# Layer 0 window attention: softmax denominators out of the value products, inverted once a step and applied one step later

## The chip, the core and the metric

The kernel runs on one core of one Trainium2 chip. The metric is the device time of one execution in microseconds (us). TensorE, VectorE, ScalarE and GpSimd work in parallel beside SyncE, which issues DMA transfers; each engine works through its own list of instructions in order, and semaphores order the engines among each other. The profile calls them PE (and PEld for TensorE's weight loads), DVE, ACT, POOL and SP.

## What is computed

A chain of four layers on an image tensor of 4 x 16 x 512 x 512 float32 values. Layer 0 is a transformer block on windows of 8 x 8 pixels; layers 1 to 3 are 3x3 convolutions with batch normalisation, residuals and a small per-pixel network. The change lies wholly in layer 0:

```python
pos = conv3x3_depthwise(x); x = x + pos + pos_b
win = windows_of_8x8(affine(x))                 # 64 tokens, 16 channels
q, k, v = split(win @ qkv_w.T + qkv_b)          # 2 heads of 8
attn = softmax(q * 8**-0.5 @ k.T, axis=-1)
out = (attn @ v) @ proj_w.T + proj_b
x = x + out
x = x + gelu(affine(x) @ fc1_w.T + fc1_b) @ fc2_w.T + fc2_b
```

## The kernel before

**Tiling.** `window_attention` puts 8 strips of the image by 16 channels on the 128 partitions and walks over the image in `STEPS` = 64 steps. A step is 4 images (`u`) by 4 pairs of strips (`vv`) by 8 windows; two windows (the two strips of a pair) lie side by side on 128 token partitions. Within a step the attention runs over eight groups `k`, and the pieces of neighbouring groups are interleaved by hand. The order on PE, DVE, ACT and SP is the order in which the program writes the instructions (`manual_schedule`); only POOL is left to a scheduler.

**A group.** `scores(k)` multiplies keys and queries (L355) into four PSUM banks, 0 to 3, and two ACT instructions take the exponential of them into a tile `e` (L363). `values(k)` transposes the input on PE (L342) and DVE copies it to `yt` (L347). `attend(k-1)` makes 16 products of 128x32 tiles over 128 columns (L374: the weights are `yt`, whose half that belongs to the other window is zero) and then four of 128x32 tiles over 512 columns with a matrix of ones, `own` (L379). The latter are the softmax denominators, repeated over the 16 channels of each window. Even groups use banks 4 and 5, odd ones 6 and 7. `divide(k-1)` inverts the denominators on ACT as exp(-ln d) (L388, L389), and DVE multiplies products and inverses into `o` (L390).

**The rest of a step.** `turn_keys` copies keys of the next step from `y` to `y2` by DMA within SBUF, 8 transfers at every odd `k`, 32 a step, all on SP's queue (L314). `queries` prepares `g` for the next step (L324, L332, L334). `project` applies the output matrix and adds the residual (L398, L403). Then follows the hidden phase: 16 `hidden` blocks, products at L411 and a Gelu on ACT at L416, woven into the `depthwise` convolution (L291) of the step after next, whose result `position` writes to `y` (L302, L306). `output` multiplies by the second matrix (L422), DVE adds the residual into `xo` (L427). In every second step `store` writes `xo` to DRAM by 64 DMA transfers on SP's queue (L92). In the kernel before, all of `output` of a step is done early in the next step. The input tiles come by DMA as well (L190): 32 loads, one for two steps.

All DMA transfers use eight completion semaphores in turn, so that one is issued only after the transfer eight places ahead of it has landed.

Of the kernel before, what the change touches and what calls it, by code (L numbers as in the profile page):

```python
# [25 lines left out]
P = 128  # L26
# [122 lines left out]
def window_attention(ctx: ExitStack, tc, xw, x1, hots, m, v, peak):  # L149
# [33 lines left out]
    def quad(i):  # L183
        return slice(32 * i, 32 * i + 32)
# [1 line left out]
    xin = ctx.enter_context(tc.tile_pool(name="w0i", bufs=2))  # L186

    def load(k):
        t = xin.tile([P, V, WS + 2, XW + 2], F32, tag="x", name=f"x{k}")
        nc.sync.dma_start(t, xw[k])  # L190
        return t

    xts, ys = {0: load(0), 1: load(1)}, {}
    hot = wts.tile([P, 64], F32, name="hot")
    nc.sync.dma_start(hot, hots)
    small, own = hot[:, 0:32], hot[:, 32:64]

    def prod(lhsT, rhs, name, n=P):

# [73 lines left out]

    y2 = pa.tile([P, V, NJ, 2, T], F32, name="y2")
    nc.gpsimd.memset(y2, 0.0)
    g = pa.tile([P, V, NJ, NH, T], F32, name="g")
    o = pa.tile([P, V, NJ, NH, T], F32, name="o")
    most = pa.tile([P, STEPS], F32, name="most")

    def by_window(ap):  # L280
# [5 lines left out]
    def depthwise(n, tap, u):  # L286

        dy, dx = divmod(tap, 3)
        at = BW * (n % 2) + dx
        for vv in range(V):  # L290
            nc.tensor.matmul(  # L291
                bank(u)[quad(vv)], taps[quad(u), tap, :],
                xts[n // 2][quad(u), vv, dy : dy + WS, at : at + BW],
                start=tap == 0, stop=tap == 8,
            )

    def position(n):

        y = px.tile([P, U, N], F32, tag="y", name=f"y{n}", bufs=3)
# [37 lines left out]
    def values(k, n):  # L337

        vv, jl = k // 2, 4 * (k % 2)
        b = bank(4 + 2 * (k % 2))  # L340
        for jj in range(4):
            nc.tensor.transpose(  # L342
                b[:, P * jj : P * jj + P],
                y2[:, vv, jl + jj].rearrange("p w t -> p (w t)"), m("ident"),
            )
        t = px.tile([P, 4, P], F32, tag="yt", name=f"yt{n}_{k}", bufs=3)
        nc.vector.tensor_copy(t.rearrange("p j c -> p (j c)"), b)  # L347
        return t

    def scores(k, n):  # L350

        vv, jl = k // 2, 4 * (k % 2)
        for jj in range(4):
            for u in range(U):
                nc.tensor.matmul(  # L355
                    bank(u)[:, P * jj : P * jj + P],
                    y2[quad(u), vv, jl + jj].rearrange("p w t -> p (w t)"),
                    g[quad(u), vv, jl + jj].rearrange("p h t -> p (h t)"),
                    start=True, stop=True,
                )  # L360
        e = px.tile([P, U, 4, P], F32, tag="e", name=f"e{n}_{k}", bufs=3)
        for i in range(2):
            nc.scalar.activation(  # L363
                e[:, 2 * i : 2 * i + 2].rearrange("p u j t -> p u (j t)"),
                pairs[i], AF.Exp,
            )
        return e

    def attend(e, yt, k):

        b, d = bank(4 + 2 * (k % 2)), bank(5 + 2 * (k % 2))
        for jj in range(4):
            for u in range(U):
                nc.tensor.matmul(  # L374
                    b[quad(u), P * jj : P * jj + P], yt[:, jj, quad(u)], e[:, u, jj, :],
                    start=True, stop=True,
                )
        for u in range(U):
            nc.tensor.matmul(  # L379
                d[quad(u)], own, e[:, u].rearrange("p j t -> p (j t)"),  # L380
                start=True, stop=True,
            )

    def divide(k, n):
        vv, jl = k // 2, 4 * (k % 2)
        b, d = bank(4 + 2 * (k % 2)), bank(5 + 2 * (k % 2))
        r = px.tile([P, 512], F32, tag="r", name=f"r{n}_{k}")
        nc.scalar.activation(r, d, AF.Ln)  # L388
        nc.scalar.activation(r, r, AF.Exp, scale=-1.0)  # L389
        nc.vector.tensor_tensor(  # L390
            o[:, vv, jl : jl + 4].rearrange("p j h t -> p (j h t)"), b, r, ALU.mult
        )

    def project(y):
        for h in range(NH):
            for u in range(U):
                for vv in range(V):
                    nc.tensor.matmul(  # L398
                        bank(4 + u)[quad(vv)], wo[h][quad(u)], o[quad(u), vv, :, h, :],
                        start=h == 0, stop=h == 1,  # L400
                    )
        for u in range(U):
            nc.vector.scalar_tensor_tensor(  # L403
                y[:, u], bank(4 + u), pb, y[:, u], ALU.add, ALU.add
            )

    def hidden(y, q, vv, n):

        u, b = q // 4, bank(4 + q % 4)
        for k in range(4):  # L410
            nc.tensor.matmul(  # L411
                b[quad(k)], fc1[quad(vv), quad(k)], y[quad(vv), u, :],
                start=True, stop=True,
            )
        hd = px.tile([P, N], F32, tag="hid", name=f"hid{n}_{u}_{vv}", bufs=16)
        nc.scalar.activation(hd, b, AF.Gelu, bias=f1b)  # L416
        return vv, hd

# [61 lines left out]
    for n in range(2):  # L480
        for tap in range(9):
            for u in range(U):
                depthwise(n, tap, u)
        ys[n] = position(n)
    for vv in range(V):
        turn_keys(ys[0], vv)
    for h in range(NH):
        queries(ys[0], h)
    last, xo = None, None
    nc.scalar.preload_act_table_set("natural_log_exp_and_others")  # L490
    for n in range(STEPS):
        yts = {k: values(k, n) for k in range(2)}
        es = {0: scores(0, n)}
        if last:

            output(*last)
        for k in range(1, 8):
            es[k] = scores(k, n)
            attend(es[k - 1], yts[k - 1], k - 1)
            if k > 1:  # L500
                yts[k] = values(k, n)
            divide(k - 1, n)
            if k == 3:
                nc.vector.tensor_reduce(
                    most[:, n : n + 1], ys[n], AX.XY, ALU.max, apply_absolute_value=True
                )
            elif largest:
                largest.pop(0)()
            if k % 2 and n + 1 < STEPS:
                turn_keys(ys[n + 1], k // 2)  # L510
        if n + 1 < STEPS:
            queries(ys[n + 1], 0)
        attend(es[7], yts[7], 7)
        divide(7, n)
        if n + 1 < STEPS:
            queries(ys[n + 1], 1)
        y = ys.pop(n)
        project(y)

        ahead = n + 2 < STEPS  # L520
        if ahead and n % 2 == 0 and n // 2 + 2 < STEPS // 2:
            xts[n // 2 + 2] = load(n // 2 + 2)
        if n % 2 == 0:
            xo = px.tile([P, U, WS, XW], F32, tag="xo", name=f"xo{n}", bufs=1)
        if n + 1 == STEPS:
            flag = bounded()

# [3 lines left out]
        hids, taken = [], [0] * U  # L531
        for i in range(13 * 4):
            if i in at:
                q = len(hids)
                hids.append(hidden(y, q, i % 4, n))
                if n + 1 == STEPS and q in (5, 9, 13):
                    u = q // 4 - 1
                    output(y, xo, hids[q - 5 : q - 1], (u,), (u,), n)
            elif ahead:
                depthwise(n + 2, taken[i % 4], i % 4)  # L540
                taken[i % 4] += 1
        if n + 1 < STEPS:
# [3 lines left out]
        last = (y, xo, hids, range(U), (5, 7, 4, 6), n)  # L546
    output(y, xo, hids[12:], (3,), (3,), n)
    for f in largest:
        f()
    return nc.values_load(flag[0:1, 0:1], min_val=0, max_val=1)  # L550
# [676 lines left out]
def _pack(a):  # L1227
# [67 lines left out]
    own = np.zeros((2, 64, 2, C))  # L1295
    for w in range(2):
        own[w, :, w, :] = 1.0
    hots = np.concatenate(
        [np.tile(np.eye(32), (4, 1)), own.reshape(P, 32)], axis=1
    ).astype(np.float32)  # L1300


    padded = np.zeros((B, C, H + 2, W + 2), np.float32)
    padded[:, :, 1 : H + 1, 1 : W + 1] = a["x"]
    xw = np.zeros((WS, 4, B, 2, C, 4, WS + 2, P + 2), np.float32)
    for i in range(WS):
        for cb in range(4):
            for strip in range(8):
                vv, w = divmod(strip, 2)
                r = H // 8 * strip + WS * i  # L1310
                xw[i, cb, :, w, :, vv] = padded[
                    :, :, r : r + WS + 2, P * cb : P * cb + P + 2
                ]
    return {
        "x": a["x"].reshape(B * C, H, W),
        "xw": xw.reshape(4 * WS, P, 4, WS + 2, P + 2),
        "mats": mats,
        "vecs": vecs,
        "cqs": cws[:, 3].reshape(P, 6 * 32),
# [26 lines left out]
```

## Time and profile before

| | us |
|---|---|
| median of 3 runs | 6030.73 (6027.56 to 6033.05) |
| the profiled execution, its own time | 6030.1 |
| its span, first to last instruction | 6028.3 |
| PE busy | 5775.3 (96%) |
| ACT busy | 3837.6 (64%) |
| DVE busy | 3268.4 (54%) |
| POOL busy | 171.1 (3%) |
| granted TensorE clock, mean | 0.993 |

Layer 0 takes the first 3440 us or so of the span; the rest is layers 1 to 3. A row of the costliest groups reads: line, engine, operation, tile written <- tiles read, shapes, how many, busy us and mean ns of one, idle time of the engine before them and what ended it. SP's instructions are all issues and waits and do not count as busy: SP has no row in the first part of the page, and has to be read from the timeline and from the durations of its issues.

### The profile page before, as it was taken

The numbers are of one execution on the slowest core, as the hardware profiler recorded it, in microseconds if no ns is written. First come the engines' busy times: TensorE is split into PE (matmuls) and PEld (weight loads), VectorE is DVE, ScalarE is ACT, GpSimd is POOL, SyncE is SP. The second block draws the span as 40 slices with busy tenths as digits, with TensorE's granted clock in tenths as the row PEclk, the third lists the DMA queues.
The fourth block names the chain that finished last, engine by engine and source line by source line (L and its number), as shares of the span: only waits on it lengthen the run. The fifth ranks groups of instructions, "written<-read, shape, count | busy, mean of one in ns | idle before, by whom it ended". The sixth has DMA issues, their size and how long they took to land. (4 is left out here: it accounts for less than half of the span.)

```text
span 6028.3 us, 242228 instructions
## 1 busy us (share of the span) xinstructions
PE 5775.3 (96%) x108624; PEld 3084.9 (51%) x108624; DVE 3268.4 (54%) x4648; ACT 3837.6 (64%) x5257; POOL 171.1 (3%) x193
## 2 busy tenths in 40 slices
PE   8999999999999999999999866899999999999999
PEld 5666666666666666666666433333333333333333
DVE  3444444444444444444444455566666666666666
ACT  4777877877787777778777654344444444444444
POOL 0000000000000000000000154000000000000000
PEclk9999999999999999999999999999999999999999
DMA  3233333323333232333333398666676666666663
GB/s 84 58 71 66 64 77 62 78 59 71 67 64 77 61 79 59 71 66 65 77 61 61 58 243 216 163 171 168 167 173 165 168 172 166 168 171 168 167 170 104
DMA packets 638119, 674.57 MB, mean 112 GB/s; under 512 B 371728, under 2 KB 500880, under 8 KB 632976
## 3 DMA queue, kind: packets, MB, share of 16 engines
q1 hardware_dynamic: 635760, 657.53, 47.1%
q8 instruction: 857, 14.04, 1.0%
q0 software_dynamic: 1024, 1.05, 0.1%
q14 instruction: 190, 1.56, 0.1%
q10 hardware_dynamic: 288, 0.39, 0.0%
HBM read 221.15 MB, written 134.48 MB: 59 GB/s over the span
## 5 line engine op out<-in xcount | busy, mean ns | idle before, releaser
L363 ACT ACTIVATE e<-pair 128x1024 f32<-128x1024 f32 x1024 | 992.5, 1021 | 381.7 <-PE pair L355 381.7
L1175 ACT ACTIVATE hid<-tb,vec 128x512 f32<-128x512 f32 x1024 | 620.7, 688 | 517.5 <-PE tb L1167 517.4
L291 PE MATMUL pair<-x,taps 32*32 32x512 f32 x18432 | 927.4, 605 | 2.6 <-ACT y L302 1.2
L1177 DVE TENSOR_SCALAR hid<-tb,vec 128x512 f32<-128x512 f32 x1024 | 695.7, 742 | 2.7 <-PE tb L1167 2.6
L411 PE MATMUL bank<-y,fc_e 32*32 32x512 f32 x8192 | 680.1, 598 | 0.9 <-DVE y L403 0.9
L355 PE MATMUL pair<-g,y 32*128 32x128 f32 x16384 | 653.0, 285 | 26.9 <-ACT y L302 25.0
L355 PEld LDWEIGHTS pair<-g,y 32*128 32x128 f32 x16384 | 542.8, 186 | 215.9 <-issue 108.9
L416 ACT ACTIVATE hid<-bank,f1b 128x512 f32<-128x512 f32 x1024 | 644.5, 686 | 12.4 <-PE bank L411 4.8
L291 PEld LDWEIGHTS pair<-x,taps 32*32 32x32 f32 x18432 | 602.2, 103 | 98.2 <-issue 19.0
L347 DVE COPY yt<-bank 128x512 f32<-128x512 f32 x512 | 347.3, 688 | 540.2 <-PE bank L342 531.9
L1167 PE MATMUL tb<-ye,mat 32*128 32x512 f32 x4096 | 637.6, 624 | 0.3 <-DVE hid L1177 0.3
L374 PE MATMUL bank<-e,yt 128*32 128x128 f32 x16384 | 556.7, 276 | 3.4 <-issue 2.4
L390 DVE TENSOR_TENSOR o<-bank,r 128x512 f32<-128x512 f32 x512 | 354.2, 692 | 372.6 <-ACT r L389 356.3
L379 PE MATMUL bank<-e,hot 128*32 128x512 f32 x4096 | 535.6, 593 | 0.0
L1187 PE MATMUL tb<-hid,mat 128*32 128x512 f32 x4096 | 466.0, 595 | 41.6 <-DVE hid L1177 41.6
L374 PEld LDWEIGHTS bank<-e,yt 128*32 128x32 f32 x16384 | 418.0, 109 | 111.7 <-DVE yt L347 52.8
L306 DVE TENSOR_SCALAR y<-pair,vec 128x512 f32<-128x512 f32 x128 | 90.3, 746 | 706.5 <-PE pair L291 706.5
L1167 PEld LDWEIGHTS tb<-ye,mat 32*128 32x128 f32 x4096 | 267.0, 183 | 323.3 <-issue 219.9
L342 PEld LDWEIGHTS bank<-mat,y 128*128 128x128 f32 x2048 | 216.3, 141 | 376.1 <-issue 270.0
L1092 PE MATMUL tb<-zo,cw 64*32 64x512 f32 x3096 | 362.8, 594 | 14.9 <-issue 8.9
L1092 PE MATMUL tb<-xo,cw 64*32 64x512 f32 x3096 | 366.1, 600 | 10.1 <-issue 7.0
L1092 PE MATMUL tb<-xe,cw 64*32 64x512 f32 x3072 | 361.5, 600 | 0.0
(176 smaller groups left out, 7564.1 us busy)
## 6 DMA issues: line engine op xcount, KB each, us to landing
x<-in_xw_dram SPq DMA_DIRECT2D x32, 2600.0 KB, 10.9
zo<-ze SPq DMA_DIRECT2D x512, 128.5 KB, 2.4
ho<-he SPq DMA_DIRECT2D x512, 128.5 KB, 2.4
xo<-xe SPq DMA_DIRECT2D x512, 128.5 KB, 2.4
y<-y SPq DMA_DIRECT2D x2048, 32.0 KB, 2.2
tx<-x SPq DMA_DIRECT2D x256, 256.0 KB, 4.6
out_dram<-xe SPq DMA_DIRECT2D x128, 512.0 KB, 3.5
x<-xo SPq DMA_DIRECT2D x2016, 32.0 KB, 1.7
```

The costliest lines, as they stand in the source:

```text
L291: nc.tensor.matmul(bank(u)[quad(vv)], taps[quad(u), tap, :], xts[n // 2][quad(u), vv, dy : dy + WS, at : at + BW], start=tap == 0, stop=ta ...
L355: nc.tensor.matmul(bank(u)[:, P * jj : P * jj + P], y2[quad(u), vv, jl + jj].rearrange("p w t -> p (w t)"), g[quad(u), vv, jl + jj].rearra ...
L363: nc.scalar.activation(e[:, 2 * i : 2 * i + 2].rearrange("p u j t -> p u (j t)"), pairs[i], AF.Exp,)
L374: nc.tensor.matmul(b[quad(u), P * jj : P * jj + P], yt[:, jj, quad(u)], e[:, u, jj, :], start=True, stop=True,)
L379: nc.tensor.matmul(d[quad(u)], own, e[:, u].rearrange("p j t -> p (j t)"), start=True, stop=True,)
L411: nc.tensor.matmul(b[quad(k)], fc1[quad(vv), quad(k)], y[quad(vv), u, :], start=True, stop=True,)
L416: nc.scalar.activation(hd, b, AF.Gelu, bias=f1b)
L1092: nc.tensor.matmul(p[r][_quad(2 * f + w)], weights[_half(r), odd, dx, :], src[_half(r), f, dx : dx + W], start=dx == 0, stop=dx == 2,)
L1167: nc.tensor.matmul(p[q], w1[_quad(q), 1 - par, :], inner(src)[_quad(q), f, :], start=True, stop=True,)
L1175: nc.scalar.activation(hd, p[q], AF.Relu, bias=v("l3_b1"))
L1177: nc.vector.tensor_scalar(hd, p[q], v("l3_b1"), 0.0, ALU.add, ALU.max)
L1187: nc.tensor.matmul(p[r][_quad(c)], w2[:, par], hd, start=(r, c) not in seen, stop=(r, c) in seen,)
```

## The change

**Denominators.** The matrix of ones is no longer multiplied. Instead `values` adds a pattern `other` to the transposed block on DVE: ones in that half of the weights which was zero, the half of the other window's channels. `attend` makes 32 products of 64x32 tiles over 128 columns in place of 16 + 4 products: window 0 goes to the even bank of the pair, as 16 rows of values and 16 equal rows of sums; window 1 to the odd bank, as 16 rows of sums and 16 of values.

**Gathering.** For each group DVE copies both banks to SBUF (`o` and a new tile `t`, four buffers). Two DMA transfers take one row of sums for each image into a tile `sums` (4 x 2 KB each), and four transfers (`merge`, 16 x 2 KB each, one group later) carry window 1's values from `t` into `o`. All six are on SP's queue.

**Inversion.** ACT's logarithm and exponential work once a step on `sums`, at the start of the next step. There DVE spreads the inverse of each group over the partitions (`stream_shuffle` into `r`) and POOL multiplies it into `o`. So `project`, `hidden` and `output` of a step come one step later, and there is a 65th pass of the loop for the last.

**Buffers and order.** `o` has two buffers, `y` four in place of three, `e` two in place of three, `hid` eight in place of sixteen. Input tiles hold one step in place of two, so there are 64 loads of half the size. Half of `output` is done in the hidden phase, the other half early in the next step. The reductions for the largest values (`most`, `peak`) move from the groups to the time after `project`.

```diff
@@ values
-        nc.vector.tensor_copy(t.rearrange("p j c -> p (j c)"), b)
+        nc.vector.tensor_tensor(
+            t.rearrange("p j (u c) -> p (j u) c", u=U),
+            b.rearrange("p (a c) -> p a c", c=32),
+            other.unsqueeze(1).to_broadcast([P, 4 * U, 32]), ALU.add,
+        )
@@ attend
-        b, d = bank(4 + 2 * (k % 2)), bank(5 + 2 * (k % 2))
+        p = bank(4 + 2 * (k % 2)), bank(5 + 2 * (k % 2))
         for jj in range(4):
             for u in range(U):
-                nc.tensor.matmul(
-                    b[quad(u), P * jj : P * jj + P], yt[:, jj, quad(u)], e[:, u, jj, :],
-                    start=True, stop=True,
-                )
+                for w in range(2):
+                    half = slice(64 * w, 64 * w + 64)
+                    nc.tensor.matmul(
+                        p[w][quad(u), P * jj : P * jj + P],
+                        yt[half, jj, quad(u)], e[half, u, jj, :],
+                        start=True, stop=True,
+                    )
...
+    def gather(o, k, n):
+        b = part(o, k)
+        t = px.tile([P, 512], F32, tag="t", name=f"t{n}_{k}", bufs=4)
+        nc.vector.tensor_copy(b, bank(4 + 2 * (k % 2)))
+        nc.vector.tensor_copy(t, bank(5 + 2 * (k % 2)))
+        d = sums[n % 2]
+        nc.sync.dma_start(d[2 * k : P : 32], b[C:P:32])
+        nc.sync.dma_start(d[2 * k + 1 : P : 32], t[0:P:32])
+        merges.append((b, t))
+    def merge():
+        b, t = merges.pop(0)
         for u in range(U):
-            nc.tensor.matmul(
-                d[quad(u)], own, e[:, u].rearrange("p j t -> p (j t)"),
-                start=True, stop=True,
-            )
-    def divide(k, n):
-        vv, jl = k // 2, 4 * (k % 2)
-        b, d = bank(4 + 2 * (k % 2)), bank(5 + 2 * (k % 2))
+            at = slice(32 * u + C, 32 * u + 2 * C)
+            nc.sync.dma_start(b[at], t[at])
+    def invert(n):
+        d = sums[n % 2]
+        nc.scalar.activation(d, d, AF.Ln)
+        nc.scalar.activation(d, d, AF.Exp, scale=-1.0)
+    def divide(o, k, n):
         r = px.tile([P, 512], F32, tag="r", name=f"r{n}_{k}")
-        nc.scalar.activation(r, d, AF.Ln)
-        nc.scalar.activation(r, r, AF.Exp, scale=-1.0)
-        nc.vector.tensor_tensor(
-            o[:, vv, jl : jl + 4].rearrange("p j h t -> p (j h t)"), b, r, ALU.mult
-        )
+        nc.vector.stream_shuffle(r, sums[n % 2], [2 * k] * C + [2 * k + 1] * C)
+        b = part(o, k)
+        nc.gpsimd.tensor_tensor(b, b, r, ALU.mult)
@@ the loop over steps
+    for n in range(STEPS + 1):
+        old = os.get(n - 1)
...
         if last:
             output(*last)
+        if old is not None:
+            invert(n - 1)
+            divide(old, 0, n - 1)
         for k in range(1, 8):
+            if n < STEPS:
+                es[k] = scores(k, n)
+                attend(es[k - 1], yts[k - 1], k - 1)
+                if k > 1:
+                    yts[k] = values(k, n)
+                gather(o, k - 1, n)
+                if k > 1:
+                    merge()
+                if k % 2 and n + 1 < STEPS:
+                    turn_keys(ys[n + 1], k // 2)
+            if old is not None:
+                divide(old, k, n - 1)
         if n + 1 < STEPS:
             queries(ys[n + 1], 0)
-        attend(es[7], yts[7], 7)
-        divide(7, n)
+        if n < STEPS:
+            attend(es[7], yts[7], 7)
+            gather(o, 7, n)
+            for _ in range(2):
+                merge()
         if n + 1 < STEPS:
             queries(ys[n + 1], 1)
...
+                if q == 9:
+                    output(y, xo, hids[:8], (0, 1), (6, 7), done)
...
+        if loads:
+            xts[loads] = load(loads)
+        last = (y, xo, hids[8:], (2, 3), (5, 7), done) if old is not None else None
```

More of the change, by code (lines that the diff above doesn't have):

```diff
@@ L188, in load @@
     def load(k):
-        t = xin.tile([P, V, WS + 2, XW + 2], F32, tag="x", name=f"x{k}")
+        t = xin.tile([P, V, WS + 2, BW + 2], F32, tag="x", name=f"x{k}")
         nc.sync.dma_start(t, xw[k])
@@ L195, in window_attention @@
     nc.sync.dma_start(hot, hots)
-    small, own = hot[:, 0:32], hot[:, 32:64]
+    small, other = hot[:, 0:32], hot[:, 32:64]
     def prod(lhsT, rhs, name, n=P):
@@ L275, in window_attention @@
     nc.gpsimd.memset(y2, 0.0)
+    sums = [pa.tile([P, 512], F32, name=f"sums{i}") for i in range(2)]
+    for d in sums:
+        nc.gpsimd.memset(d, 1.0)
     g = pa.tile([P, V, NJ, NH, T], F32, name="g")
-    o = pa.tile([P, V, NJ, NH, T], F32, name="o")
     most = pa.tile([P, STEPS], F32, name="most")
@@ L288, in depthwise @@
         dy, dx = divmod(tap, 3)
-        at = BW * (n % 2) + dx
         for vv in range(V):
@@ L292, in depthwise @@
                 bank(u)[quad(vv)], taps[quad(u), tap, :],
-                xts[n // 2][quad(u), vv, dy : dy + WS, at : at + BW],
+                xts[n][quad(u), vv, dy : dy + WS, dx : dx + BW],
                 start=tap == 0, stop=tap == 8,
@@ L297, in position @@
     def position(n):
-        y = px.tile([P, U, N], F32, tag="y", name=f"y{n}", bufs=3)
+        y = px.tile([P, U, N], F32, tag="y", name=f"y{n}", bufs=4)
         for u in range(U):
@@ L360, in scores @@
                 )
-        e = px.tile([P, U, 4, P], F32, tag="e", name=f"e{n}_{k}", bufs=3)
+        e = px.tile([P, U, 4, P], F32, tag="e", name=f"e{n}_{k}", bufs=2)
         for i in range(2):
@@ new lines, in part @@
+    def part(o, k):
+        vv, jl = k // 2, 4 * (k % 2)
+        return o[:, vv, jl : jl + 4].rearrange("p j h t -> p (j h t)")
+    def gather(o, k, n):
[7 more added lines that the diff above has]
+        merges.append((b, t))
@@ L392, in divide, with highest, project @@
+    def highest(n):
+        nc.vector.tensor_reduce(
+            most[:, n : n + 1], ys[n], AX.XY, ALU.max, apply_absolute_value=True
         )
-    def project(y):
+    def project(y, o):
         for h in range(NH):
@@ L414, in hidden @@
             )
-        hd = px.tile([P, N], F32, tag="hid", name=f"hid{n}_{u}_{vv}", bufs=16)
+        hd = px.tile([P, N], F32, tag="hid", name=f"hid{n}_{u}_{vv}", bufs=8)
         nc.scalar.activation(hd, b, AF.Gelu, bias=f1b)
@@ L484, in window_attention @@
         ys[n] = position(n)
+        xts[n + 2] = load(n + 2)
     for vv in range(V):
@@ L488, in window_attention @@
         queries(ys[0], h)
-    last, xo = None, None
+    highest(0)
+    last, xo, os, merges = None, None, {}, []
     nc.scalar.preload_act_table_set("natural_log_exp_and_others")
-    for n in range(STEPS):
-        yts = {k: values(k, n) for k in range(2)}
-        es = {0: scores(0, n)}
+    for n in range(STEPS + 1):
+        old = os.get(n - 1)
+        if n < STEPS:
+            o = os[n] = pa.tile([P, V, NJ, NH, T], F32, tag="o", name=f"o{n}", bufs=2)
+            yts = {k: values(k, n) for k in range(2)}
+            es = {0: scores(0, n)}
@@ L494, in window_attention @@
         if last:
             output(*last)
+        if old is not None:
+            invert(n - 1)
+            divide(old, 0, n - 1)
         for k in range(1, 8):
[L498 to L505, printed above, removed]
-                )
-            elif largest:
-                largest.pop(0)()
@@ L509, in window_attention @@
-            if k % 2 and n + 1 < STEPS:
-                turn_keys(ys[n + 1], k // 2)
+            if n < STEPS:
[10 more added lines that the diff above has]
+                divide(old, k, n - 1)
@@ L511, in window_attention @@
         if n + 1 < STEPS:
             queries(ys[n + 1], 0)
-        attend(es[7], yts[7], 7)
-        divide(7, n)
+        if n < STEPS:
+            attend(es[7], yts[7], 7)
+            gather(o, 7, n)
+            for _ in range(2):
+                merge()
         if n + 1 < STEPS:
             queries(ys[n + 1], 1)
[L517 to L522, printed above, removed]
@@ L523, in window_attention @@
-        if n % 2 == 0:
-            xo = px.tile([P, U, WS, XW], F32, tag="xo", name=f"xo{n}", bufs=1)
         if n + 1 == STEPS:
             flag = bounded()
+        ahead = n + 2 < STEPS
+        if ahead and n + 4 < STEPS:
+            loads = n + 4
+        else:
+            loads = None
+        done = n - 1
+        if old is not None:
+            y = ys.pop(done)
+            project(y, os.pop(done))
+        if n + 1 < STEPS:
+            highest(n + 1)
+        if old is not None:
+            while largest:
+                largest.pop(0)()
+            if done % 2 == 0:
+                xo = px.tile([P, U, WS, XW], F32, tag="xo", name=f"xo{done}", bufs=1)
@@ L533, in window_attention @@
             if i in at:
+                if old is None:
+                    continue
                 q = len(hids)
[L535 to L538, printed above, removed]
+                hids.append(hidden(y, q, i % 4, done))
+                if q == 9:
+                    output(y, xo, hids[:8], (0, 1), (6, 7), done)
             elif ahead:
@@ L541, in window_attention @@
                 taken[i % 4] += 1
+            if i in (34, 44) and largest:
+                largest.pop(0)()
         if n + 1 < STEPS:
@@ L545, in window_attention @@
             ys[n + 2] = position(n + 2)
-        last = (y, xo, hids, range(U), (5, 7, 4, 6), n)
-    output(y, xo, hids[12:], (3,), (3,), n)
+        if loads:
+            xts[loads] = load(loads)
+        last = (y, xo, hids[8:], (2, 3), (5, 7), done) if old is not None else None
+    output(*last)
     for f in largest:
@@ L1293, in _pack @@
     cws = np.tile(np.concatenate([cws, cws[:, :, ::-1]]), (2, 1, 1, 1, 1))
-    own = np.zeros((2, 64, 2, C))
+    other = np.ones((2, 64, 2, C))
     for w in range(2):
-        own[w, :, w, :] = 1.0
+        other[w, :, w, :] = 0.0
     hots = np.concatenate(
-        [np.tile(np.eye(32), (4, 1)), own.reshape(P, 32)], axis=1
+        [np.tile(np.eye(32), (4, 1)), other.reshape(P, 32)], axis=1
     ).astype(np.float32)
@@ L1304, in _pack @@
     padded[:, :, 1 : H + 1, 1 : W + 1] = a["x"]
-    xw = np.zeros((WS, 4, B, 2, C, 4, WS + 2, P + 2), np.float32)
+    xw = np.zeros((WS, 8, B, 2, C, 4, WS + 2, P // 2 + 2), np.float32)
     for i in range(WS):
-        for cb in range(4):
+        for cb in range(8):
             for strip in range(8):
@@ L1311, in _pack @@
                 xw[i, cb, :, w, :, vv] = padded[
-                    :, :, r : r + WS + 2, P * cb : P * cb + P + 2
+                    :, :, r : r + WS + 2, P // 2 * cb : P // 2 * cb + P // 2 + 2
                 ]
@@ L1315, in _pack @@
         "x": a["x"].reshape(B * C, H, W),
-        "xw": xw.reshape(4 * WS, P, 4, WS + 2, P + 2),
+        "xw": xw.reshape(8 * WS, P, 4, WS + 2, P // 2 + 2),
         "mats": mats,
```

## The prediction

> **What bounds the kernel now.** I read the timeline of layer 0 first, because the change touches one group of a step and nothing after 3440 us. This is one group `k`:
>
> ```profile
> 1503.17 0.98 PEld L355 LDWEIGHTS pair<-g,y 32*128 32x128 f32 x32 [0.17 <-issue]
> ...
> 1504.27 1.08 PE L374 MATMUL bank<-e,yt 128*32 128x128 f32 x32
> 1504.38 1.94 ACT L363 ACTIVATE e<-pair 128x1024 f32<-128x1024 f32 x2 [0.40 <-PE pair L355]
> 1505.06 0.24 PEld L379 LDWEIGHTS bank<-e,hot 128*32 128x32 f32 x8
> ...
> 1506.14 0.42 PEld L342 LDWEIGHTS bank<-mat,y 128*128 128x128 f32 x4 [0.84 <-issue]
> ...
> 1506.28 0.60 ACT L388 ACTIVATE r<-bank 128x512 f32<-128x512 f32 x1
> 1506.73 0.98 PEld L355 LDWEIGHTS pair<-g,y 32*128 32x128 f32 x32 [0.17 <-issue]
> ```
>
> The group is 3.56 us from `scores` to `scores`, and PE goes from one product to the next: scores 1.10, values 0.79 (1504.27 to 1505.06), denominators 1.08 (to 1506.14), transposes 0.59. ACT idles 0.40 us in it, waiting for PE. So **PE is the bound of the groups**. The step's length comes from the instructions that read the projection, four a step:
>
> ```profile
> L403 DVE SCALAR_TENSOR_TENSOR y<-bank,pb,y x256: 739/743/752, 102.7 to 3426.4; 128x512 f32<-128x512 f32 x128
> ```
>
> From the first at 102.7 to the first of step 63 (3426.4 less 3 x 0.68) are 63 steps: **52.7 us a step**.
>
> Then I read SP, which has no busy row, because the change adds transfers. These are its issues, first in the lists by line (duration of one: least, median, most, in ns), then in the timeline of SP (start, length, how many):
>
> ```profile
> L314 SPq DMA_DIRECT2D y<-y x2048: 585/598/2127, 44.6 to 3401.1; - x187
> ```
> ```profile
> L92 SPq DMA_DIRECT2D x<-xo x2016: 302/424/2115, 175.7 to 3448.3; - x184
> ```
> ```profile
> L1037 SPq DMA_DIRECT2D zo<-ze x256: 507/590/1282, 3761.0 to 5938.7; - x128
> ```
> ```profile
> 1379.87 17.72 SPq L314 DMA_DIRECT2D y<-y  x24
> ...
> 1398.33 28.16 SPq L314 DMA_DIRECT2D y<-y  x32
> 1441.93 34.58 SPq L92 DMA_DIRECT2D x<-xo  x64
> ```
>
> An issue holds SP for 0.42 to 0.60 us, and some hold it over 2 us. With the gaps and the long ones, 24 `turn_keys` transfers took 17.72 us, 0.74 each; 64 stores took 34.58, and the next batch 36.12 (timeline at 1547): 0.55 each. Two steps hold 64 + 64 of them and one load at 0.6: 47.4 + 35.2 + 0.6 = **83.2 us of the 105.4 us of two steps**. SP is not a bound now, but it is 79% taken.
>
> [...] 0.60 us of issue against the 2.2 us that the page shows to landing, and issues follow one another while landings overlap. [...]
>
> **The change part by part.**
>
> *PE.* In L374 each column tile takes 8 of the 32 instructions in 0.79 us. The change has 64 instructions (every fp32 product is two) on eight tiles, again 8 on each: 0.79 us if eight run at once; 1.6 us if they only follow each other at L374's pace (0.79/32 each). The denominators' 1.08 us go. So PE's group falls from 3.56 to 2.5, at worst 3.3. I take 2.5.
>
> *ACT.* It loses L388 and L389, 8 x (0.596 + 0.630) = 9.8 us a step, and gains 1.2 once. But scores and exponential wait for each other: the banks 0 to 3 are single. At 1552.02 in the timeline `scores` of a group starts as the exponential before it ends, and the exponentials then stand 3.08 us apart (1550.28, 1553.36). So a group can't go below about 3.1 us, and PE's 1.08 is worth about 0.45 a group, 3 us over the seven of a step.
>
> *DVE.* Four instructions a group in place of two: the addition in `values` and two copies at 0.69 (L347's 688 ns, L390's 692), and the shuffle. [...]
>
> *POOL.* One product of two SBUF tiles a group. [...] The trace has only one-input work there (L980, 1024 columns in 1.12 us). It has a whole step of time; only above 6 us each would it matter.
>
> *SP.* Each group adds two transfers for `sums` and four for `merge`, 48 a step; loads double to one a step. No row shows 4 x 2 KB or 16 x 2 KB within SBUF. The nearest are layer 3's shifts within SBUF, 0.507 at least and 0.59 in the median. In the timeline at 5010 twelve of them start within 8.4 us, 0.70 each with waits; pairs without waits, 0.61 each. I take **0.66**, between these. The low end is a store's unstalled 0.47 (0.424 and the gap), say 0.5; the high end that of `turn_keys` at 0.74. Two steps then hold 47.4 + 35.2 + 1.2 + 96 x 0.66 = 63.4: **147.2 us of issues against 105.4 us that the steps last now.** That doesn't fit, so SP becomes the bound.
>
> *How it binds.* In SP's order a step is: two `sums` transfers, 8 `turn_keys`, then two and four, two and four and 8, and so on, 80 transfers, some 55 us, where the engines need 25 us for the groups. `t` has four buffers, so DVE's copy of group 6 waits for the merge of group 2, that of group 7 for the merge of group 3. Behind these copies stand, on DVE, the queries of the next step and the residual of `project`; PE waits for the banks, then ACT. After the merge of group 3 SP still has 38 transfers, 16 x 0.74 + 22 x 0.66 = 26.4, and a load. The engines take, from the copy of group 7 to the first `sums` transfer of the next step, what the trace shows from 1526.45 (end of L390) to about 1552.5: 26 us, plus the landing of 2.2. So in a step without stores SP rests 2 to 3 us; in a step with stores it never rests, as 32 of them are due in the hidden phase and 32 early in the next step, ahead of the first `sums` transfer. I add 3 us for this rest and 1.5 for waits behind the loads (1.3 MB; the 2.6 MB ones took 10.9 us to land): 151.7 us for two steps, **75.9 a step**.
>
> *Ends.* The 65th pass adds an inversion (1.2)[...] and about 4 of hidden work that no convolution covers: 15 us.
>
> *Sum.* 64 x (75.9 - 52.7) = 1485, and 15: 1500 over the profiled execution's 6030.1, that is **7530 us**. The median, 6030.73, is the same within 0.6.
>
> **The rivals.**
>
> *SP binds, at another price (part of the forecast).* At 0.5 us an issue: 47.4 + 35.2 + 1.2 + 48 + 3 = 134.8, 67.4 a step, 6985 us. At 0.74, with `turn_keys` at 0.78 and 6 us of rest: 50 + 35.2 + 1.2 + 71 + 7.5 = 164.9, 82.5 a step, 7950 us.[...]
>
> *Faster: SP keeps up.* Then the groups' 3 us a step are won: 6030 - 64 x 3 + 15 = 5850 us. For this the 96 transfers must fit into 2 x 49.7 - 83.8 = 15.6 us, 0.16 us each. The least issue of all rows is 0.302. I see nothing for it but that small transfers were never seen: 4%.
>
> *No gain, no loss.* 0.22 us an issue; no mechanism holds it there: 1%.
>
> *It doesn't do what it says.* If 64x32 products don't run eight at once, a group is 3.3 on PE instead of 3.1: under SP's bound this changes nothing, and without it it leaves about 6030 - 64 x 1.5 + 15 = 5950.
>
> *POOL or DVE binds.* Above 6 us for a POOL product the groups would take 8 x 6 and more. This would come on top only past SP's 75.9 a step, which needs 9 us each. I give it 2%, at 8000 and more.
>
> **How the numbers follow.** SP as the bound has 93%. Its own ends are 6985 and 7950; the likeliest value is 7530, and I give 7000 to 7900 for eight times in ten. A measurement of this kernel tells about 0.2%, 12 us, from no change. Faster 4%, same 1%, slower 95%.
>
> **What would show it.** Right: in the timeline SP's issues of layer 0 follow without a pause for most of a step; the new transfers' issue is 0.5 to 0.7; the first instruction of `project` comes every 76 us; PE's share in layer 0 falls to about 65%, and its long waits end on DVE's copy into `t` or on a DMA. The denominators' 1.08 us are gone, and PE's weights for 64x32 tiles take about 0.8 us a group. Wrong: issues at 0.3 or less, or a step below 60 us; a step of about 50 us means that SP kept up; long waits that end on POOL's product mean that POOL binds.

## The result, and the profile after

The changed kernel takes 7587.92 us in the median (7585.23 to 7591.73, four runs), the kernel before 6030.62 in the same comparison: a ratio of 1.2583, 95% interval 1.2561 to 1.2605. The profiled execution took 7591.7 us, its span is 7589.8, its mean granted clock 0.876 where it was 0.993.

The first two parts of the page after (busy time; then PE and the clock in 40 slices):

```profile
PE 5751.7 (76%) x120912; PEld 3145.4 (41%) x120912; DVE 3895.8 (51%) x6184; ACT 3315.0 (44%) x4363; POOL 822.0 (11%) x707
...
PE   7676676656675677656675676666899999999999
...
PEclk8888788878887888878887888779999999999999
```

Layer 0 fills the first 26 slices, and no engine reaches 80% in them. PE does about as many microseconds of work as before (5775.3) in a longer time. Something that has no busy row sets the end. The step, from the residual of `project` (least, median and most ns, first and last start):

```profile
L434 DVE SCALAR_TENSOR_TENSOR y<-bank,pb,y x256: 740/743/754, 170.1 to 4986.5; 128x512 f32<-128x512 f32 x128
```

(4986.5 - 3 x 0.68 - 170.1) / 63 = **76.4 us a step**. That is read as before. It is a mean of 63 unlike steps: in DVE's timeline they alternate, some 61 us without stores and some 94 with them, and the last one, in the 65th pass, which has no groups, took 35.7 (4948.83 to 4984.53). Without it the mean is 77.1. In the kernel before the steps take 52.7 to 54.3 us, and the last one 47.8. The timeline of SP, from one load to the load two steps later (start, length, how many):

```profile
1514.85 0.37 SPq L190 DMA_DIRECT2D x<-in_xw_dram  x1
1515.32 17.54 SPq L92 DMA_DIRECT2D x<-xo  x32
1532.96 0.56 SPq L398 DMA_DIRECT2D sums<-o  x1
1533.62 0.53 SPq L399 DMA_DIRECT2D sums<-t  x1
1534.26 5.39 SPq L315 DMA_DIRECT2D y<-y  x8
1539.74 0.57 SPq L398 DMA_DIRECT2D sums<-o  x1
1540.41 0.56 SPq L399 DMA_DIRECT2D sums<-t  x1
1541.07 2.48 SPq L406 DMA_DIRECT2D o<-t  x4
...
1581.62 5.55 SPq L406 DMA_DIRECT2D o<-t  x8
1587.27 0.53 SPq L190 DMA_DIRECT2D x<-in_xw_dram  x1
1590.42 0.55 SPq L398 DMA_DIRECT2D sums<-o  x1
...
1642.48 5.59 SPq L406 DMA_DIRECT2D o<-t  x8
1648.17 20.11 SPq L92 DMA_DIRECT2D x<-xo  x32
1668.38 0.37 SPq L190 DMA_DIRECT2D x<-in_xw_dram  x1
```

In these 153.5 us each transfer is issued at the end of the one before, mostly within 0.1 us. There is one rest of over half a microsecond, from 1587.80 to 1590.42, in the step that has no stores behind it. From 300 to 4800 us all gaps of over 0.3 us sum to 170 us, some 4% of the time, and waits for the landing of earlier transfers are among them. (In the kernel before, of 3207 issues from 300 to 3300 us none ends before the transfer eight places ahead of it has landed, and 26 before the one seven places ahead has.) So it is the issues themselves that fill the time: SP is the bound. The durations of its issues, by line:

```profile
L398 SPq DMA_DIRECT2D sums<-o x512: 503/563/637, 78.6 to 4950.0; - x171
```
```profile
L406 SPq DMA_DIRECT2D o<-t x2048: 527/587/1887, 87.2 to 4955.7; - x187
```

How the engines feel it is in the list of waits (us in total, times, longest us; 100 to 4990 us):

```profile
POOL o L418 <- DVE r L416: 3115.8, 371, 37.9
ACT g L333 <- DVE g L335: 1841.7, 126, 46.5
DVE t L396 <- DMA o<-t: 1560.0, 203, 36.0
PEld bank L381 <- DVE yt L348: 1041.9, 65, 35.0
```

The root is the third line: DVE's copy into `t` waits for a merge, 1560 us in 203 stops. Behind it on DVE stand `queries` (ACT's wait) and the addition into `yt` (PE's wait). The first line, the largest, is the idle time of an engine that is 11% busy and costs nothing.

Between the stops the groups run as follows. One group, in PE's weights:

```profile
1603.97 1.25 PEld L360 LDWEIGHTS pair<-g,y 32*128 32x128 f32 x32 [0.17 <-issue]
1605.34 0.91 PEld L381 LDWEIGHTS bank<-e,yt 64*32 64x32 f32 x64
1606.45 0.42 PEld L343 LDWEIGHTS bank<-mat,y 128*128 128x128 f32 x4 [0.20 <-issue]
1607.04 1.26 PEld L360 LDWEIGHTS pair<-g,y 32*128 32x128 f32 x32 [0.17 <-issue]
```

The denominators are gone and the group is 3.07 us long (1603.97 to 1607.04), against 3.56. The 64 products of 64x32 tiles take 1.11 us to the next transposes; in 0.20 of it no weights are loaded.

### The profile page after: what moved, and what is told of

Read it like the earlier page. It is cut to its first block, busy times and chain, and to the rows that moved or that the text cites. A ratio compares the mean times of both kernels' runs of the same rounds, so it can differ in the third digit from the quotient of the medians.

```text
span 7589.8 us, 274615 instructions
## 1 busy us (share of the span) xinstructions
PE 5751.7 (76%) x120912; PEld 3145.4 (41%) x120912; DVE 3895.8 (51%) x6184; ACT 3315.0 (44%) x4363; POOL 822.0 (11%) x707
## 5 line engine op out<-in xcount | busy, mean ns | idle before, releaser
L381 PE MATMUL bank<-e,yt 64*32 64x128 f32 x32768 | 641.1, 286 | 1039.1 <-DVE yt L348 1009.8
L396 DVE COPY t<-bank 128x512 f32<-128x512 f32 x512 | 351.1, 686 | 1572.1 <-DMA o<-t 1567.7
L418 POOL TENSOR_TENSOR o<-o,r 128x512 f32<-128x512 f32 x512 | 650.2, 1271 | 4298.1 <-DVE r L416 3115.8
L333 ACT ACTIVATE g<-pair,gb 128x512 f32<-128x512 f32 x256 | 172.4, 688 | 1847.8 <-DVE g L335 1847.8
L381 PEld LDWEIGHTS bank<-e,yt 64*32 64x32 f32 x32768 | 488.9, 110 | 1175.9 <-DVE yt L348 1046.9
L360 PE MATMUL pair<-g,y 32*128 32x128 f32 x16384 | 777.9, 290 | 50.5 <-ACT e L368 23.9
L360 PEld LDWEIGHTS pair<-g,y 32*128 32x128 f32 x16384 | 647.0, 188 | 222.2 <-ACT e L368 111.6
L325 PE MATMUL pair<-y,wg 32*32 32x512 f32 x4096 | 275.2, 915 | 514.9 <-ACT g L333 513.4
L348 DVE TENSOR_TENSOR yt<-bank,hot 128x512 f32<-128x512 f32 x512 | 346.6, 687 | 300.3 <-PE bank L343 298.1
L416 DVE STREAM_SHUFFLE r<-sums 128x512 f32<-128x512 f32 x512 | 375.0, 733 | 0.6
```

The lines of the kernel that those rows point to most:

```text
L360: nc.tensor.matmul(bank(u)[:, P * jj : P * jj + P], y2[quad(u), vv, jl + jj].rearrange("p w t -> p (w t)"), g[quad(u), vv, jl + jj].rearra ...
L381: nc.tensor.matmul(p[w][quad(u), P * jj : P * jj + P], yt[half, jj, quad(u)], e[half, u, jj, :], start=True, stop=True,)
L418: nc.gpsimd.tensor_tensor(b, b, r, ALU.mult)
```

## The experiments

In each kernel a step is the mean of 63 from the residual of `project`, as above; with the step of delay the last of them is a short one everywhere (35 to 37 us). The kernel before was run beside all of them (6024 to 6027 us in the median). A figure without a ratio is a single execution.

### The issues alone, without the change

The kernel before gets 48 transfers a step on SP, of the same shapes and in the same places, into a tile that nobody reads. `e` has two buffers in place of three, for room. 

```diff
+        nc.sync.dma_start(spare[2 * k : P : 32], src[C:P:32])
+        nc.sync.dma_start(spare[2 * k + 1 : P : 32], src[0:P:32])
...
+        for u in range(U):
+            at = slice(32 * u + C, 32 * u + 2 * C)
+            nc.sync.dma_start(spare2[at, k % 2], src[at])
```

> The kernel before, with 48 transfers a step of the same two sizes within SBUF added on SP's queue at the same places (two of 4 x 2 KB and four of 16 x 2 KB a group) into a spare tile that nobody reads; e has two buffers in place of three to make room. Theory A: SP's issues alone make 74.4 us a step and some rest: 6030 + 64 x 23 = 7500 us, 7350 to 7650. Theory B: nobody waits for these transfers, so only turn_keys come a little later: 6030 to 6150 us.

Measured: 7453.21 us, a step of 75.1. The change costs 1557 us, and the issues alone cost 1427, with four buffers of `t`, the inversion, POOL's products and the 64x32 products all absent. The wait is another one here (200 to 4800 us):

```profile
PE bank L344 <- DMA spare<-o: 486.0, 26, 20.1
```

L344 is the transposes of `values`, which read what `turn_keys` brought. In the timeline PE stops before them for 17 us, until 1600.46, and the eight `turn_keys` transfers that they need are issued from 1593.24 to 1598.64; the list puts the wait down to a spare transfer that was issued beside them. So nobody waits for `t` here, and the step is nearly the same: SP's queue sets it by whatever is waited for in the queue.

A smaller dose tells whether the cost is proportional or begins at a threshold: only the two transfers for `sums` a group, 16 a step.

```diff
-        for u in range(U):
-            at = slice(32 * u + C, 32 * u + 2 * C)
-            nc.sync.dma_start(spare2[at, k % 2], src[at])
```

> The kernel before with 16 transfers a step of 4 x 2 KB added on SP's queue, read by nobody (e with two buffers, as in e4). Theory A: 42 + 16 x 0.66 = 52.6 us a step on SP just reach the 52.7 us of the engines; with a rest 53.5 to 55.5 a step: 6080 to 6210 us. If each added issue cost its share of e4's loss whatever the room on SP (1427 us for 48): 6030 + 476 = 6500 us.

Measured: 6168.03 us, ratio 1.0248 (1.0221 to 1.0274), a step of 54.8. A third of the transfers costs a tenth of the loss. With 83.2 + 32 x 0.66 = 104.3 us of issues in two steps SP stands just at the 105.4 of the kernel before, so the cost begins at a threshold. In DVE's timeline the steps without stores still take 52.7 us, and only those with stores are longer (53.0 to 61.6). That also shows that the two buffers of `e` cost nothing in this kernel as long as SP keeps up.

### The change without its transfers

All 48 transfers a step are left out. So `sums` keeps ones and window 1's values are left out of the result. The work of PE, ACT, DVE and POOL is that of the change.

```diff
-        nc.sync.dma_start(d[2 * k : P : 32], b[C:P:32])
-        nc.sync.dma_start(d[2 * k + 1 : P : 32], t[0:P:32])
...
-            nc.sync.dma_start(b[at], t[at])
```

> The changed kernel without its 48 new transfers a step: left out are the gathering of the sums (sums stay ones, so nothing is divided) and window 1's values in o. All else of the change stays, on the same engines: 64x32 products, copies, inversion, shuffles, products on POOL, the step of delay. Theory A (only the issues made it slow): SP has its 42 us of before, and the engines set the step. From e7, where a step without a transfer in the way lasted 53.2 us, I expect 52 to 54 us a step: 6000 to 6150 us, within 2% of the kernel before. Theory B (the longer chain of inverting, shuffling and multiplying, or the products themselves): it stays above 6300 us.

Measured: 6058.43 us, ratio 1.0056 (1.004 to 1.0073), a step of 52.8. From the other side again: the transfers carry all of the loss but some 35 us (6058.43 less the 6023.76 beside it). But the 3 us a step that the groups should give don't appear either. The wait list of this kernel (200 to 3300 us), and of the kernel before, for the products of `attend`:

```profile
PE bank L381 <- issue: 59.0, 46, 3.3
```
```profile
PE bank L374 <- issue: 2.4, 4, 1.2
```

PE stops inside a burst of 64 products though the list shows nothing that it waits for. The timeline of one such stop, PE's weights:

```profile
1502.47 0.79 PEld L381 LDWEIGHTS bank<-e,yt 64*32 64x32 f32 x50
1506.12 0.22 PEld L381 LDWEIGHTS bank<-e,yt 64*32 64x32 f32 x14 [2.86 <-issue]
1506.72 0.71 PEld L343 LDWEIGHTS bank<-mat,y 128*128 128x128 f32 x4 [0.39 <-issue]
```

This stop costs more than its length: the granted clock is 1.00 from 1499.3 to 1502.5 and 0.57 from 1506 to 1510, and the weights of four transposes (L343) take 0.71 us in place of 0.42.

The DMA view of 1498 to 1508 has in it the input load of 1320 KB, which keeps the DMA engines over 90% busy for most of 1501.5 to 1505, and two packets of the queue that the page calls "instruction". This queue (q8) is read as the one that brings PE's instructions: it has 953 packets in this run and 857 in the kernel before, one for 254 instructions of PE and PEld in both. From 200 to 3300 us PE's weights stop 42 times for over 1 us with the reason "issue", and each stop ends 1.2 to 1.8 us after the end of a packet of this queue; a time chosen at random would lie so in 12 of 100 cases. So these stops are read as PE waiting for its instructions.

To see whether the load is what stops PE, the same kernel was run without input loads except the first two: the input of 62 steps is left out as well.

```diff
-            xts[loads] = load(loads)
+            xts[loads] = xts[loads - 2]
```

> As e11 (no new transfers), and without the loads of the input tiles but the first two: the convolutions of all later steps read these two again (left out: the input of 62 steps). In e11 PE stops in the middle of a group for 0.8 to 3.2 us in most steps and goes on at 'issue', while the DMA engines are busy with the 1.3 MB load of a step; steps without such a stop last 50.5 us, the mean 53.15. Theory C (the load in flight delays what PE needs to go on, its own instructions, fetched by DMA): the stops vanish, 50.5 to 51.5 us a step: 5890 to 5960 us, below the kernel before. If the stops come from the 64x32 products themselves: 6040 to 6080, as e11.

Measured: 5928.08 us, ratio 0.9831 (0.9816 to 0.9846), a step of 50.6. Its wait list, the same line:

```profile
PE bank L381 <- issue: 2.6, 6, 0.8
```

No stop of over 1 us is left. At the three lines of the groups (L381, L360, L343) PE's stops with the reason "issue" sum to 3.2 us, where the kernel with loads has 96.6. The time is 130 us less; the slower products behind each stop fit the rest, which was not taken apart.

The load alone is not enough. In the kernel before one of 2600 KB is in flight in the group that the prediction shows (the window, then PE, PEld, DVE, ACT and POOL busy, clock, DMA share, GB/s):

```profile
1503.17:1506.73 3.56, 3.56 (x77) 2.43 (x77) 1.38 (x2) 3.13 (x5) 0.00 (x0) 1.00 0.98 333
```

PE doesn't stop there. It has 152 instructions, weights and products, in the 3.56 us of that group; the changed one has 200 in 3.07. That PE uses its instructions up faster than they come in beside a load fits both; the time from the request of a packet to its landing was not seen. The kernel before was not run without its loads; PE is 99% busy in its layer 0 (3122.5 of 3150 us), so it has little to win there.

### More buffers for t

```diff
-        t = px.tile([P, 512], F32, tag="t", name=f"t{n}_{k}", bufs=4)
+        t = px.tile([P, 512], F32, tag="t", name=f"t{n}_{k}", bufs=6)
```

> The changed kernel with six buffers of t in place of four. Theory A (SP's issue time sets the step): the copies into t wait later, but SP has the same 149 us of issues in two steps; only the rest of 3 us in every second step can shrink: 7490 to 7600 us. Theory B' (the four buffers throttle the groups, and SP merely follows): two more groups run ahead, and 10 us or more a step are won: below 7000 us.

Measured: 7538.2 us, ratio 1.2506 (1.2482 to 1.2529), a step of 75.9. So the copies' wait for `t`, though it is the root in the wait list, is only where SP's delay comes in. Two more buffers take away part of SP's rest, 50 us: its gaps of over 0.3 us fall from 3.8 to 2.7% of the time (300 to 4700 us here). The rate of issue stays.

### Sharing the issues with POOL

Three kernels move part of SP's list to POOL's queue. The stores:

```diff
-                    slice(XW * cb, XW * cb + XW), queues if k == STEPS // 2 - 1 else None,
+                    slice(XW * cb, XW * cb + XW),
+                    queues if k == STEPS // 2 - 1 else itertools.repeat(nc.gpsimd),
```

> The changed kernel with the stores of xo (64 in two steps) issued from POOL's queue in place of SP's. Theory A (SP's issue time sets the step): SP keeps 112 issues less 32 a step: two steps hold 64 x 0.74 + 96 x 0.67 + 1.2 = 113 us of issues, 56.6 a step, with a rest of some 3 us a step before the first sums transfer 59.5 us a step; time about 7588 - 64 x (76.4 - 59.5) = 6510 us, 6400 to 6650. Theory B (the new waits set it: sums must land, be inverted, shuffled and multiplied before project[...]; SP's own load only goes along): nothing of that chain changes, 7400 to 7600 us.

Measured: 7000.32 us, a step of 67.0; 490 us more than expected. The timeline of POOL shows why:

```profile
1599.96 15.12 POOL L92 DMA_DIRECT2D x<-xo  x30 [15.83 <-DVE xo L458]
1616.36 0.51 POOL L92 DMA_DIRECT2D x<-xo  x1 [1.28 <-DMA x<-xo]
1617.56 16.60 POOL L92 DMA_DIRECT2D x<-xo  x33 [0.69 <-DMA x<-xo]
1634.18 3.72 POOL L418 TENSOR_TENSOR o<-o,r 128x512 f32<-128x512 f32 x3
```

POOL first waits for `xo`, then issues 64 stores until 1634.16, and only then come products. DVE's shuffle needs a buffer of `r` back from a product, so it waits too (475.9 us in 27 stops from 300 to 4000 us, up to 20.2). One queue was relieved and another, with work that is waited for, got a block of 34 us.

The merges, and then all 48 transfers, on POOL:

```diff
-            nc.sync.dma_start(b[at], t[at])
+            nc.gpsimd.dma_start(b[at], t[at])
```

> The changed kernel with the 32 merge transfers a step on POOL's queue. Theory A: SP has 32 x 0.74 + 32 x 0.55 + 16 x 0.66 + 0.6 = 52.5 us a step, with a rest 54 to 56; 7588 - 64 x 21.4 = 6220 us, 6100 to 6350. Theory B: the wait of DVE's copy into t for the merge stays, now for a transfer from POOL, 7400 us or more. If a POOL issue takes over 1 us, POOL has 32 + 10 us a step, still no bound.

Measured: 6746.69 us, a step of 63.2; over 500 us more than expected. POOL's merges can't run ahead of SP (300 to 4000 us):

```profile
POOL o L406 <- DMA sums<-o: 805.1, 166, 15.3
```

A merge overwrites rows of `o` behind the transfer that reads a row of sums from it, and that one still stands in SP's list behind the stores. In DVE's timeline the steps alternate, some 53 us without stores and 74 with them.

```diff
-        nc.sync.dma_start(d[2 * k : P : 32], b[C:P:32])
-        nc.sync.dma_start(d[2 * k + 1 : P : 32], t[0:P:32])
+        nc.gpsimd.dma_start(d[2 * k : P : 32], b[C:P:32])
+        nc.gpsimd.dma_start(d[2 * k + 1 : P : 32], t[0:P:32])
...
-            nc.sync.dma_start(b[at], t[at])
+            nc.gpsimd.dma_start(b[at], t[at])
```

> The changed kernel with all 48 new transfers a step on POOL's queue. Theory A: SP is back at 42 us a step, and the engines set the step: 50 to 51 us, so 7588 - 64 x 26 = 5925 us, 5850 to 6030, a little below the kernel before; POOL has 48 x 0.52 + 8 x 1.27 = 35 us a step. If an issue on POOL takes 1 us, POOL is the bound at 58 us a step: 6400 us. Theory B: 7400 us or more.

Measured: 6724.03 us, ratio 1.1147 (1.1128 to 1.1166), a step of 63.0. In SP's timeline there is now a rest of 6.5 us ahead of a load (1560.96 to 1567.44), 5.6 behind it and 21 after the next `turn_keys`, so SP no longer binds. POOL's timeline in the groups:

```profile
1528.04 2.01 POOL L406 DMA_DIRECT2D o<-t  x4 [0.91 <-DMA sums<-o]
1530.04 0.57 POOL L398 DMA_DIRECT2D sums<-o  x1
1530.61 0.57 POOL L399 DMA_DIRECT2D sums<-t  x1
1531.21 1.28 POOL L418 TENSOR_TENSOR o<-o,r 128x512 f32<-128x512 f32 x1
1533.37 2.01 POOL L406 DMA_DIRECT2D o<-t  x4 [0.88 <-DMA sums<-o]
```

A transfer holds POOL for 0.49 to 0.58 us in the median (merges, `sums`), much as it holds SP. A group is 2.01 + 2 x 0.57 + 1.28 = 4.4 us of POOL, and 5.3 with the waits for earlier transfers to land (0.91), against 3.1 on the other engines. POOL also releases `project`, in the wait list of this kernel (200 to 4000 us):

```profile
PEld bank L429 <- POOL o L418: 306.8, 60, 8.9
```

5.1 us in each step. So this is the prediction's sign of a bound by POOL, brought about by issues and not by the products, which kept their 1.28. That would be half of the 10.2 us by which the step exceeds that without transfers; the other half was not taken apart.

### Fewer, wider transfers

If the number of issues is the price, twelve transfers a step should cost a quarter of 48 with the same bytes. `t` becomes as large as `o`. After the last group eight transfers of 8 x 2 KB fill `sums`, and four of 16 x 16 KB do the merging.

```diff
-            nc.sync.dma_start(b[at], t[at])
+            nc.gpsimd.dma_start(flat(o)[at], flat(t)[at])
```

On POOL:

> The changed kernel with t as large as o (one buffer for a whole step) and the 48 transfers of a step made as 12 wide ones after the last group: 8 for sums (one row of 16 KB each, spread to 8 rows), 4 for merge (16 x 16 KB each), all on POOL's queue, where the hidden phase leaves POOL idle. Theory A, and that POOL's order was what kept e1 to e3 above their forecasts: SP has its 42 us a step as before the change, POOL 8 x 1.27 + 12 x 0.5 = 16 us, so the engines set the step: groups of 3.1 us in place of 3.56 make 50 to 51 us: 5860 to 5950 us, faster than the kernel before by 1 to 3%. If the chain of inverting, shuffling and multiplying costs a step of its own (theory B): above 6100 us.

Measured: 6184.52 us, ratio 1.0272 (1.025 to 1.0294), a step of 54.8. Of the 1557 us lost 1403 come back, but there is no gain over the kernel before. On SP:

> As e7, with the 12 wide transfers on SP's queue. Theory A: the number of issues counts and not the bytes: 23.7 + 17.8 + 0.6 + 12 x 0.66 = 50.0 us a step on SP, with a rest of some 3 us 52 to 54 us a step: 6000 to 6130 us. If bytes in flight were what held SP (the same 1.1 MB a step as in the changed kernel), above 7000 us.

Measured: 6634.0 us, ratio 1.1021 (1.0997 to 1.1044), a step of 61.4; over 500 us more than expected. SP's timeline over two steps:

```profile
1491.85 20.22 SPq L92 DMA_DIRECT2D x<-xo  x32
1512.17 24.44 SPq L315 DMA_DIRECT2D y<-y  x32
...
1542.28 6.02 SPq L416 DMA_DIRECT2D o<-t  x4
1548.35 2.26 SPq L190 DMA_DIRECT2D x<-in_xw_dram  x1
1550.72 28.83 SPq L315 DMA_DIRECT2D y<-y  x32
...
1590.96 23.05 SPq L92 DMA_DIRECT2D x<-xo  x32
```

Two steps have 154 issues, against 226 in the changed kernel, but SP has no rest in these 122 us, and from 300 to 3900 us its gaps of over 0.3 us sum to only 150. So SP is the bound here too, and the price of an issue has gone up: a `turn_keys` transfer takes 0.76 and 0.90 us here, where 0.74 was put, a store 0.63 and 0.72 (0.55), a wide merge 1.5 (0.66), a load up to 2.3. The queue's own delay then reaches ACT, since the twelve stand at the end of a step's list and the next step's inversion waits for them in every second step (348.4 us in 30 stops from 200 to 4000 us, up to 15.8).

The longer issues are not a matter of SP's own wide transfers. Where POOL issues these, a `turn_keys` transfer on SP still takes 0.92 us in the mean, gaps of over 0.3 us left out, and 0.74 in the changed kernel. The DMA engines are busier in both wide forms (0.45 and 0.47 of the time in layer 0, 0.29 in the changed kernel). That this is the cause was not tested by itself.

Two attempts to gain what the wide form on POOL still lacked. One moves DVE's copies of group 6 and the shuffle of group 7 behind the evacuation of the first half of `queries`:

```diff
-                gather(o, k - 1, n)
+                if k < 7:
+                    gather(o, k - 1, n)
...
+            gather(o, 6, n)
```

> As e7 (12 wide transfers on POOL), with DVE's copies of group 6 and the shuffle for group 7 moved behind the queries' evacuation in DVE's order. In e7 the stretch from the first queries' products to project is 5.4 us against 3.7 in the kernel before, since DVE comes late to the queries. If that is where the groups' gain goes, 1.6 us a step come back: 6184 - 100 = 6080 us, 6040 to 6130, still not below the kernel before. If PE was held by something else there, 6170 to 6200.

Measured: 6191.82 us, ratio 1.0284 (1.0249 to 1.032). No gain: from `queries` to `project` PE needs 4.05 us a step in place of 4.95, but from `project` to the next `values`, the hidden phase, 22.5 in place of 21.8. Without transfers the hidden phase is 19.4. In the wide form on POOL PE stops in it as well, in the products of `depthwise` (1000 to 3000 us):

```profile
PE pair L292 <- issue: 26.8, 20, 3.2
```

The kernel without transfers has no such row. Of all stops of over 1 us at "issue" in the wide form, 91 of 97 again end 1.2 to 1.8 us after a packet of PE's instructions. The other splits each load into four parts, spread over the groups:

```diff
-            xts[loads] = load(loads)
+            pieces = [(loads, vv) for vv in range(V)]
...
+                    nc.sync.dma_start(xts[j][:, vv], xw[j][:, vv])
```

> As e7 (12 wide transfers on POOL, nothing left out), with each load of an input tile split into four of 0.33 MB, issued on SP at every odd group of the next step. Theory C: shorter loads hold PE up less, up to 1.5 us a step come back; the wide merges still hold it up in the hidden phase: 6184 - 100 = 6085 us, 6020 to 6150. If splitting doesn't help since the same bytes are in flight: 6170 to 6200.

Measured: 6190.15 us, ratio 1.0266 (1.0252 to 1.0281). No gain, though the splitting does what it was made for: from 200 to 3500 us PE's stops at "issue" in L381 fall from 61.8 to 10.0 us. But SP, with four loads a step to issue and `turn_keys` at 0.94 us each, has hardly a rest any more: its gaps of over 0.3 us sum to 14 of 3200 us, against 321 in the form that is not split. So SP may set the step again; a kernel with the split loads on another queue was not run. No kernel that computes the whole result beat the kernel before.

## Why the prediction was right

**SP as the bound: right, and the terms held.** Means from the start of an issue to the start of the next, over SP's timeline from 300 to 4800 us, gaps of over 0.3 us counted apart: `turn_keys` 0.74 (as taken), stores 0.56 (0.55), `sums` 0.64 and merges 0.70 (0.66 for both). In two steps these lines take 47.2, 35.7, 20.4 and 44.6 us, loads 1.2: 149.1, predicted 147.2. The gaps, for which 4.5 was put as rests and waits behind loads, are 5.4. Together 154.5 against 151.7. The form held too: in the cycle shown a rest of 2.6 us in the step without stores, none in the other.

**How it binds: right.** The long waits end on DVE's copy into `t`, and the queries and `yt` stand behind it. That this place is not needed for the loss is seen in the kernel before with 48 transfers more, and with six buffers of `t`. PE is busy 3147.0 of 4700 us in layer 0 (200 to 4900), 67%; 65% was named. The clock fell to 0.82 there (1.00 before). SP's issues don't show it: a `turn_keys` transfer is 599 ns in the median, 598 before.

**The ends: wrong in form, and nearly right in size by luck.** The sum has 64 steps, each longer by 75.9 - 52.7 = 23.2 us, and a tail of 15, the author's estimate. Measured are 62 steps longer by 24.4 (77.1 less 52.7): 1510 us. The first residual comes 67.4 us later (170.1 against 102.7), since a whole pass now stands before it. The last step, the 65th pass, is 17 us shorter than before (35.7 against 52.7), since no groups are left in it. What follows is 1.4 longer. That makes the 1561.5 us between the spans within 1. Outside the 62 steps it is 52 us, where the sum has 2 x 23.2 + 15 = 61. Neither the dear pass in front nor the cheap one at the end was seen, and they nearly cancel. So the 58 us to the predicted 7530 come from the step: 62 x 1.2 = 72 us too little, less these 10.

**PE's products: right in kind.** One after another at 0.79/32 us, 64 products would take 1.6 us, and they take 1.11, with the weights in 0.91; 0.79 was taken for both. That is 17 ns for each, where L374's 32 took 25. How many of the 64x32 tiles run at once is not shown; eight was the author's estimate. The group is 3.07, where 3.1 was said to bound it. DVE's shuffle is 0.733 us and a POOL product 1.271, and no trace of before shows a price for either. In the group shown DVE is busy 2.55 and POOL 1.17 of the 3.07 us, so the work of both stays hidden.

**The rival that SP keeps up: its price was too good.** 5850 us counted 3 us a step. With no transfers at all it is 6058, and only without loads as well 5928. Two things were missed. PE stops at "issue" while a load is in flight: the step is 2.2 us longer with loads than without. And `queries` comes when DVE still has copies and a shuffle to do: from there to `project` PE needs 4.94 us without transfers, 3.85 before. Without loads the groups do become shorter, from 31.4 us a step to 26.6 (first `values` to first `queries`), but the hidden phase, which now makes half of `output`, grows from 17.6 to 19.4. So even with all its transfers free the change as it stands wins nothing (ratio 1.0056), and 1.7% when its loads are free too.

## What to carry to other kernels

Count a queue's issues as an engine's instructions: number times duration, stalls and gaps taken from the timeline, against the time that the step leaves. SP's queue, 79% taken and without a busy row, had no room for 48 transfers more a step (75.1 us a step against 52.7; with 16 more it was 54.8). Moving issues to another engine moved their price into that engine's order (64 stores held POOL for 34 us); ask who waits behind them there. Making them fewer and wider lowers their number and here raised the price of each: a merge on SP from 0.70 to 1.5 us, `turn_keys` from 0.74 to between 0.80 and 0.94. So read the durations again after such a change.

## What the runs showed of the hardware that was not expected

In the changed kernel a transfer within SBUF held SP's queue for 0.55 to 0.60 us in the median, at 8 KB (L398 and L399: 0.563 and 0.551) and at 32 KB (L406 and L315: 0.587 and 0.599) alike. On POOL's queue it was 0.49 to 0.58 with all 48 transfers there. At 256 KB it was 0.49 on POOL, but 0.5 to 4.0 on SP, 1.1 in the median. `turn_keys` on SP (32 KB) took 0.74 us in the mean in the changed kernel, 0.80 beside wide transfers on SP and 0.92 and 0.94 beside wide transfers on POOL.

In the kernel without transfers PE stopped for up to 3.4 us while an input load of 1320 KB was in flight, and each of 42 stops ended 1.2 to 1.8 us after a packet of the queue called "instruction". Without the loads no stop of over 1 us was left. The kernel before, with loads of 2600 KB, has one, of 1.5 us. Behind a stop of 2.86 us the granted clock was 0.57 where it had been 1.00.

64 products of 64x32 tiles took 17 ns each in the changed kernel, 1.11 us for a burst, where the 32 of 128x32 tiles took 25 in the kernel before.
